# A fifth dB tile in the pool of the selective scan from the first image on, and one sz tile fewer in the stage that prepares the scan

## The chip, the cores and the metric

The kernel runs on one core of one Trainium2 chip. A run's time is the device time of one execution, in microseconds (us). Engines are named as in the profile: PE (TensorE, matmuls), DVE (VectorE), ACT (ScalarE), POOL (GpSimd) and SP (SyncE, which here only issues DMAs). "L534" is line 534 of the kernel.

## What is computed

Four images of 64x64 positions with 128 channels go through four layers: a state-space block (layer 0), a global attention (layer 1), a convolution block (layer 2) and a windowed attention with an MLP (layer 3). The change is in layer 0, whose core is a scan over the 4096 positions in four directions k, for 256 channels with 16 states each:

```
def step(h, t):
    x_t, d_t, B_t, C_t = t
    h = exp(d_t[..., None] * A) * h + (d_t * x_t)[..., None] * B_t[:, :, None, :]
    return (h, einsum('bkdn,bkn->bkd', h, C_t))
```

The names in the kernel are: dA for the exponential, du for d_t * x_t, dB for du times B, and hc for h times C.

## The kernel before, in words

**Two stages in one program.** `scan_inputs` (L307) works out, for one image, what the scan reads: a layer norm, a projection, a 3x3 convolution, the gate sz = silu(z), and for each direction delta, du and the rows B and C. All of it goes to scratch in DRAM. `selective_scan` (L487) reads that back and runs the scan of one image. `network` (L1751) calls `scan_inputs` for image 0, then the scan of image 0, and behind it in the text `scan_inputs` for images 1 to 3; then, for each later image, its scan and, in the text after it, the rest of the network (`rest`, L1721) for the image before. A scheduler fixes the order of each engine's queue when the program is built, by priorities and by an estimate of times: the scan's instructions have a lower priority (`SCAN_FIRST`, L1790) than the other stages, so that they fill what the others leave free. On the chip each queue runs strictly in that order.

**A unit of the scan.** For each of 4 directions, 8 chunks of 512 positions and 2 halves of the channels there are 4 groups of states (`j`, L523) and 2 tiles (`pp`, L531): 512 units for an image, 2048 in all. One unit is:

- one dB product on POOL (L534), 128x1024, from a du tile and the B rows, into a tile that `S.inputs.tile()` gives;
- two exponentials on ACT (L540), 128x512 each, into PSUM tiles dA, of which there are three;
- two scans on DVE (L542), 128x512 each, from dA and dB;
- the C product, either two 128x512 products on DVE (L547) or one 128x1024 product on POOL (L555);
- copies of the last state on ACT (L549, L551), and four of the matmuls on PE that sum over states (L588).

Which units have their C product on POOL is set by `ON_POOL` (L57): six of sixteen in image 0, seven of sixteen later. A product on POOL is put `BEHIND` = 2 units later in the text (L557), so its priority comes after the dB product two units on. The hc tile of a unit is free again when PE has read it.

**The tiles.** The class `Tiles` (L470) hands out tiles of [128, 2, 512] in turn from one pool, and, after `widen`, from a second pool too. hc has 6 tiles in image 0 and 10 later; dB has 4 in image 0 and 5 later. `widen` sets `turn` to -40 (L477), so that the first 40 tiles after it still come from the first pool alone. A dB product waits until the two scans that read the same tile before have ended.

```
    def widen(self, pool, extra):
        self.more, self.extra, self.turn = pool, extra, -40
...
                        dB = S.inputs.tile()
                        nc.gpsimd.tensor_mul(dB, dus[pp], mid(bt, 2))
```

**sz.** In `scan_inputs`, the pool `si_a` has two buffers for a tile unless a number is given. sz (L381) is written by two silu activations on ACT (L389) for each of the eight chunks of an image, and sent to DRAM by a DMA that ACT issues (L412).

Of the kernel before, what the change touches and what calls it, by code (L numbers as in the profile page):

```python
# [28 lines left out]
F32 = mybir.dt.float32  # L29
# [11 lines left out]
ND = DI // 128  # L41
FF = 4 * C
NF = FF // 128
LC = 512
# [242 lines left out]
def token_tiles(dram, c):  # L287

    return dram[span(c), :].rearrange("(t p) c -> p t c", p=128)
# [17 lines left out]
def scan_inputs(tc, K, A, D, img):  # L307
# [5 lines left out]
    with ExitStack() as ctx:  # L313
        pool = ctx.enter_context(tc.tile_pool(name="si_a", bufs=2))
# [49 lines left out]
        for c in range(NCH + 1):  # L364
            acts = []
            if c < NCH:
                xt = pool.tile([128, 4, 128], F32, name="x")
                nc.sync.dma_start(xt, token_tiles(A["x"][img], c))
                xnT = pool.tile([128, LC], F32, name="xnT")
                layernorm_T(tc, K, pool, psum, xt, ln_w, ln_b, xnT)  # L370
                band = pool.tile([128, ND, RC + 2, W], F32, name="band", bufs=3)
                bands[c] = band
                for d in range(ND):
                    ps = psum.tile([128, LC], F32, name="ps")
                    nc.tensor.matmul(ps, in_proj[:, d * 128 : (d + 1) * 128], xnT, start=True, stop=True)
                    rows = ps.rearrange("p (h w) -> p h w", w=W)
                    nc.scalar.copy(band[:, d, 1 : RC + 1, :], rows)
                    if c > 0:
                        nc.scalar.copy(bands[c - 1][:, d, RC + 1, :], rows[:, 0, :])
                        nc.scalar.copy(band[:, d, 0, :], bands[c - 1][:, d, RC, :])  # L380
                sz = pool.tile([128, ND, LC], F32, name="sz")  # L381
                for d in range(ND):
                    ps = psum.tile([128, LC], F32, name="ps")
                    mm = nc.tensor.matmul(
                        ps, in_proj[:, DI + d * 128 : DI + (d + 1) * 128], xnT, start=True, stop=True
                    )
                    if d == 0:
                        together.open(mm)
                    acts.append(lambda d=d, ps=ps, sz=sz: nc.scalar.activation(sz[:, d, :], ps, AF.Silu))  # L389
            if c > 0:  # L390

                b, src = c - 1, bands.pop(c - 1)
                top, bottom = (1 if b == 0 else 0), (RC + 1 if b == NCH - 1 else RC + 2)
                for d in range(ND):
                    ps = psum.tile([128, LC], F32, name="ps")
                    mm = conv3x3(
                        nc,
                        ps.rearrange("p (h w) -> p h w", w=W),
                        lambda t, d=d: diag[:, d, t, :],
                        src[:, d, top:bottom, :],  # L400
                        1 - top,
                        RC,
                        bottom - top,
                    )
                    acts.append(
                        lambda d=d, ps=ps, b=b: nc.scalar.activation(
                            xc[:, d, span(b)], ps, AF.Silu, bias=conv_b[:, d : d + 1]
                        )
                    )
            together.run(mm, acts)  # L410
            if c < NCH:
                nc.scalar.dma_start(D.sz[img][c], sz)  # L412
            if c > 0:
                nc.scalar.dma_start(D.xc[img][c - 1], xc[:, :, span(c - 1)])
                steps(0, c - 1)
# [24 lines left out]
def make_scan(ctx, tc, K, A):  # L440

    nc = tc.nc
    S = SimpleNamespace()
    big = ctx.enter_context(tc.tile_pool(name="ss_big", bufs=1))
    S.pool = ctx.enter_context(tc.tile_pool(name="ss", bufs=2))
    S.psum = ctx.enter_context(tc.tile_pool(name="ss_ps", bufs=1, space=PSUM))
    load = loader(tc, big, A, 0)
    S.A = load("A_log", [128, KD, NJS, NPR, 2])
    nc.scalar.activation(S.A, S.A, AF.Exp)
    nc.vector.tensor_scalar_mul(S.A, S.A, -1.0)  # L450
    ds4 = load("Ds", [128, ND, KD])
    total = big.tile([128, ND], F32, name="Dsum")
    nc.vector.tensor_reduce(total, ds4, AX.X, ALU.add)
    S.skip = big.tile([128, ND, 128], F32, name="skip_diag")
    for d in range(ND):
        nc.scalar.activation(S.skip[:, d, :], K.ident, AF.Copy, scale=total[:, d : d + 1])

    S.pick = big.tile([128, 32], F32, name="pick")
    nc.gpsimd.memset(S.pick, 1.0)
    for base, sign in ((0, 1), (3, -1)):  # L460
        nc.gpsimd.affine_select(
            S.pick, S.pick, [[-4 * sign, 32]], ALU.is_ge, 0.0, base=base, channel_multiplier=sign
        )
    S.unit = 0
    S.products = Tiles(S.pool, "hc", 6)
    S.inputs = Tiles(S.pool, "dB", 4)
    return S


# [1281 lines left out]
def network(tc, A, out):  # L1751
    nc = tc.nc
    with ExitStack() as ctx:
        nc.scalar.preload_act_table_set("natural_log_exp_and_others")
        K = make_consts(ctx, tc)
        dram = ctx.enter_context(tc.tile_pool(name="scratch", bufs=1, space=DRAM))

        def scratch(name, shape, kind=F32):
            return dram.tile(shape, kind, name=f"{name}_dram")

        D = SimpleNamespace()
        D.bias = scratch("bias", [len(BIAS_KINDS), 128, HEADS * 512])
        D.biasT = [[scratch(f"biasT{k}_{i}", [128, HEADS, LC]) for i in range(4)] for k in range(3)]
        D.T = scratch("T", [128, HEADS * (2 * KW - 1) + 1, W])
        D.conv_diag = scratch("conv_diag", [128, ND, 9, 128])
        D.w2_norms = scratch("w2_norms", [128, len(NORMS2), 4])
        D.w2_cv4, D.w2_bias = scratch("w2_cv4", [128, 128]), scratch("w2_bias", [3, 128], BF16)
        for name, shape in (("sz", [128, ND, LC]), ("xc", [128, ND, LC]), ("y", [128, ND, LC])):
            setattr(D, name, [[scratch(f"{name}{b}_{c}", shape) for c in range(NCH)] for b in range(B)])
        for name, shape in (("delta", [128, ND, LC]), ("du", [128, ND, LC]), ("bc", [NS, 2, LC])):  # L1770
            made = [
                [[scratch(f"{name}{b}_{k}_{c}", shape) for c in range(NCH)] for k in range(KD)] for b in range(B)
            ]
            setattr(D, name, made)
        D.y_first = [[[scratch(f"y_first{b}_{k}_{c}", [128, ND, LC]) for c in range(NCH)] for k in range(2)] for b in range(B)]
        D.y_cols = [scratch(f"y_cols{b}", [NCH, 128, NCH, ND, RC * RC]) for b in range(B)]
        for name in ("x4", "x5"):
            setattr(D, name, [scratch(f"{name}_{b}", [NT, C]) for b in range(B)])
        D.shift = [scratch(f"shift{b}", [NJ, 128]) for b in range(B)]

        with ExitStack() as scan_ctx:
            S = make_scan(scan_ctx, tc, K, A)
            make_conv_diagonals(tc, K, A, D.conv_diag)
            with priority(tc, K, SCAN_FIRST // 2):
                with tc.tile_pool(name="mk_w2", bufs=1, side="right") as pool:
                    make_layer2(tc, K, A, D, pool)
            scan_inputs(tc, K, A, D, 0)
            before = None
            for img in range(B):
                with priority(tc, K, SCAN_FIRST):  # L1790
                    selective_scan(tc, K, S, D, img)
                if img == 0:
                    make_bias(tc, K, A, D)
                    for later in range(1, B):
                        scan_inputs(tc, K, A, D, later)
                    more = scan_ctx.enter_context(tc.tile_pool(name="ss_more", bufs=1))
                    S.products.widen(more, 4)
                    S.inputs.widen(more, 1)
                else:
                    rest(tc, K, A, D, img - 1, before)  # L1800
                    before = img - 1, out[img - 1]
            rest(tc, K, A, D, B - 1, before, scan_ctx.close, out[B - 1])
        needed = ctx.enter_context(tc.tile_pool(name="needed", bufs=1)).tile([1, 1], mybir.dt.int32, name="needed")
        bound_exceeded(tc, K, needed)
        with tc.If(nc.values_load(needed) > 0):
            everything_again(tc, K, A, D, out)
# [80 lines left out]
```

## Time and profile before

| what | value |
|---|---|
| median of 3 runs | 8719.03 us (8716.36 to 8720.45) |
| the profiled execution's own time | 8713.75 us |
| its span, first to last instruction | 8712.4 us |
| POOL busy | 7119.3 us (82%) |
| DVE busy | 7095.9 us (81%) |
| PE busy | 6971.9 us (80%) |
| ACT busy | 5688.0 us (65%) |
| first dB product of image 0 starts | 102.4 us |
| last du product of `scan_inputs` starts | 2046.8 us |
| last scan of image 3 starts | 7620.1 us |
| dB products on POOL, L534 | 2048, 2367 ns each |
| C products on POOL, L555 | 864, 2367 ns each |
| du products on POOL, L358 | 128, 2614 ns each |

The span is 1.35 us less than the time of the same execution, and that time is 5.28 us below the median. A row of the profile's groups gives the line, the engine, the operation, what it writes and reads, the shapes and the count; then the busy time in us and the mean of one in ns; then the engine's idle time just before these instructions, and what ended most of it. The windows give, for stretches of the span, the busy time of each engine with its number of instructions, the granted clock of PE and the share and rate of the DMAs. After 7621 us the scan is over and POOL has nearly nothing to do; the rest of the network for image 3 takes what is left of the span.

### The profile page before, as it was taken

To read this page: it belongs to the slowest core of one execution; us is meant where nothing else is said; L and a number is where in the kernel's file an instruction comes from. 1 tells how busy PE (TensorE), PEld (TensorE's weight loads), DVE (VectorE), ACT (ScalarE), POOL (GpSimd) and SP (SyncE) were. 2 spreads that over 40 slices of the span, in tenths; PEclk is the share of its full clock that TensorE was granted. 3 is DMA by queue.
4 is the path that set the end of the run, shared out by engine and by line. 5 is a ranking of instruction groups with operands and counts; after the bars stand their busy time and mean duration, and the time that the engine had idled before them with its cause. 6 is when DMAs were issued, how large, how long until landed. Compare 5 with 4: busy or idle time off the path is not lost. (4 is left out here: it accounts for less than half of the span.)

```text
span 8712.4 us, 101929 instructions
## 1 busy us (share of the span) xinstructions
PE 6971.9 (80%) x30468; PEld 2615.3 (30%) x30468; DVE 7095.9 (81%) x8477; ACT 5688.0 (65%) x11652; POOL 7119.3 (82%) x3112
## 2 busy tenths in 40 slices
PE   6758587786788878777798877777899877888978
PEld 2223132222422222233322222234322223344333
DVE  4788787788899999998899999998899999913433
ACT  5657676675666676667766676667766766654366
POOL 6989999898899989998899989998899989900000
PEclk8868687787899988888899988888999988899989
DMA  5776667676555556565455566565455565520020
GB/s 181 254 261 236 244 235 257 227 261 220 172 176 167 170 190 206 190 223 186 162 180 169 171 197 201 192 225 176 164 172 168 180 204 196 191 73 5 0 84 11
DMA packets 859647, 1562.73 MB, mean 179 GB/s; under 512 B 224446, under 2 KB 342348, under 8 KB 856781
## 3 DMA queue, kind: packets, MB, share of 16 engines
q1 hardware_dynamic: 728781, 1379.94, 47.8%
q10 hardware_dynamic: 130304, 176.19, 5.7%
q8 instruction: 244, 4.00, 0.2%
q14 instruction: 318, 2.61, 0.1%
HBM read 1286.51 MB, written 281.92 MB: 180 GB/s over the span
## 5 line engine op out<-in xcount | busy, mean ns | idle before, releaser
L534 POOL TENSOR_TENSOR dB<-du,b_rows 128x1024 f32<-128x1024 f32 x2048 | 4797.9, 2367 | 374.9 <-DVE hc L542 95.0
L540 ACT ACTIVATE dA<-dt,w_A_log 128x512 f32<-128x512 f32 x4096 | 2778.3, 690 | 509.9 <-DVE hc L542 256.7
L542 DVE TENSOR_TENSOR_SCAN dA<-dA,state,dB 128x512 f32<-128x512 f32 x2072 | 2559.9, 1272 | 295.9 <-POOL dB L534 140.4
L555 POOL TENSOR_TENSOR hc<-hc,c_rows 128x1024 f32<-128x1024 f32 x864 | 2045.3, 2367 | 73.4 <-issue 22.2
L542 DVE TENSOR_TENSOR_SCAN hc<-dA,state,dB 128x512 f32<-128x512 f32 x1512 | 1871.9, 1267 | 281.8 <-ACT dA L540 123.5
L547 DVE TENSOR_TENSOR hc<-dA,c_rows 128x512 f32<-128x512 f32 x2368 | 1522.6, 675 | 31.8 <-PE py L588 13.9
L588 PE MATMUL py<-hc,pick 128*32 128x512 f32 x8192 | 1231.0, 675 | 261.5 <-POOL hc L555 235.4
L549 ACT COPY state<-dA 128x1 f32<-128x1 f32 x2072 | 318.6, 158 | 1170.8 <-DVE hc L547 1158.9
L878 PE MATMUL pa<-e,l_v 128*128 128x512 f32 x2048 | 1069.5, 654 | 16.6 <-ACT e L834 16.1
L830 PE MATMUL pair<-l_g,l_f 32*128 32x512 f32 x2048 | 533.3, 670 | 172.6 <-ACT e L834 130.6
L834 ACT ACTIVATE e<-pair 128x1024 f32<-128x1024 f32 (+1 forms) x448 | 508.5, 1135 | 234.4 <-PE pair L830 228.0
L1019 POOL MEMSET l_h<- 64x128 f32 x8 | 1.6, 196 | 707.9 <-DVE l_h L993 707.9
L878 PEld LDWEIGHTS pa<-e,l_v 128*128 128x128 f32 x2048 | 376.3, 200 | 673.9 <-issue 624.4
L588 PEld LDWEIGHTS py<-hc,pick 128*32 128x32 f32 x8192 | 212.1, 115 | 996.5 <-issue 467.5
L277 PE MATMUL ps<-band,w_conv_diag 128*128 128x504 f32 (+3 forms) x1152 | 501.9, 595 | 6.4 <-ACT delta L427 5.7
L1404 PE MATMUL pair<-table,ident 128*128 128x512 f32 x768 | 397.3, 641 | 91.7 <-ACT e L1414 63.3
L231 PE MATMUL ps<-ident,ln_xn 128*128 128x128 f32 x512 | 144.4, 375 | 327.6 <-ACT ln_xn L228 243.9
L542 DVE TENSOR_TENSOR_SCAN dA<-dA,dB 128x512 f32<-128x512 f32 x296 | 348.2, 1211 | 45.8 <-ACT dA L540 22.0
L358 POOL TENSOR_TENSOR du<-delta,xc 128x1024 f32<-128x1024 f32 x128 | 333.4, 2614 | 47.7 <-ACT delta L427 46.7
L1414 ACT ACTIVATE e<-pair 128x1024 f32<-128x1024 f32 (+1 forms) x224 | 254.3, 1135 | 95.8 <-PE pair L1408 95.5
L277 PEld LDWEIGHTS ps<-band,w_conv_diag 128*128 128x128 f32 x1152 | 221.1, 193 | 288.0 <-issue 261.1
L830 PEld LDWEIGHTS pair<-l_g,l_f 32*128 32x128 f32 x2048 | 140.0, 189 | 530.2 <-ACT e L834 258.9
(297 smaller groups left out, 8674.4 us busy)
## 6 DMA issues: line engine op xcount, KB each, us to landing
b_rows<-bc_dram SPq DMA_DIRECT2D x1024, 256.0 KB
c_rows<-bc_dram SPq DMA_DIRECT2D x1024, 256.0 KB
dt<-delta_dram SPq DMA_DIRECT2D x512, 512.0 KB
du<-du_dram SPq DMA_DIRECT2D x512, 512.0 KB
delta_dram<-delta ACTq DMA_DIRECT2D x128, 512.0 KB
du_dram<-du SPq DMA_DIRECT2D x128, 512.0 KB
table<-biasT_dram SPq DMA_DIRECT2D x72, 512.0 KB
y_first_dram<-y_sum ACTq DMA_DIRECT2D x128, 256.0 KB
```

Of the source, the lines that this page charges most:

```text
L277: mm = nc.tensor.matmul(out[:, r0 - row0 : r1 - row0, c0:c1], lhsT((dy + 1) * 3 + dx + 1), src[:, r0 + dy : r1 + dy, c0 + dx : c1 + dx], s ...
L358: nc.gpsimd.tensor_mul(du.rearrange("p d (a b) -> p d a b", b=H), deltas[b].rearrange("p d (a b) -> p d a b", b=H), tk,)
L534: nc.gpsimd.tensor_mul(dB, dus[pp], mid(bt, 2))
L540: nc.scalar.activation(dA, dts[pp][:, g, :], AF.Exp, scale=S.A[:, k, j, pr, g : g + 1])
L542: nc.vector.tensor_tensor_scan(hg[:, order], dA[:, order], dB[:, g, order], 0.0 if i == 0 else state[:, j, pr, g : g + 1], ALU.mult, ALU.add,)
L547: mm = nc.vector.tensor_mul(hc[:, g, :], dA, ct)
L555: made.append(nc.gpsimd.tensor_mul(hc, hc, mid(ct, 2)))
L588: mm = nc.tensor.matmul(py[0][32 * q : 32 * q + 32, :], S.pick, hcs[q // 2][:, q % 2, :], start=(k == 1 and j == 0), stop=(j == NJS - 1),)
L830: nc.tensor.matmul(ps[:, u, :], f[quad, t // 4, span(t % 4, 128)], g[quad, c, :], start=True, stop=True)
L834: made = nc.scalar.activation(e, ps, AF.Exp)
L878: nc.tensor.matmul(pa, v[:, 8 * q + t, :], es[q], start=(t == 0 and q == 0), stop=(t == 7 and q == 3),)
L1404: nc.tensor.matmul(ps[:, u, :], K.ident, t[:, u, :], start=True, stop=False)
```

## The change

The pool of the scan gets five dB tiles when it is made, before image 0. The second pool, which is opened after image 0, no longer holds a dB tile; it still holds the four extra hc tiles. In `scan_inputs` sz has one tile where it had two. A dB tile and an sz tile are of one size, 4 KB in each partition, so the room that the two stages take together stays what it was.

```diff
@@ scan_inputs
-                sz = pool.tile([128, ND, LC], F32, name="sz")
+                sz = pool.tile([128, ND, LC], F32, name="sz", bufs=1)
@@ make_scan
     S.products = Tiles(S.pool, "hc", 6)
-    S.inputs = Tiles(S.pool, "dB", 4)
+    S.inputs = Tiles(S.pool, "dB", 5)
@@ network
                     S.products.widen(more, 4)
-                    S.inputs.widen(more, 1)
```

## The prediction

> **What bounds the kernel now.** I read the page first: its busy digits, 40 slices of the span.
>
> ```profile
> DVE  4788787788899999998899999998899999913433
> POOL 6989999898899989998899989998899989900000
> ```
>
> POOL and DVE share the scan's load, and POOL is near full from the second slice until the scan ends. So I cut the span into the stages of the program, in the view of windows (length, then busy time of PE, weight loads, DVE, ACT and POOL with counts, PE's granted clock, DMA share and GB/s).
>
> ```profile
> 102.00:2050.00 1948.00, 1397.03 (x4439) 488.98 (x4437) 1529.00 (x1754) 1302.08 (x2924) 1819.10 (x778) 0.77 0.71 245
> 2050.00:2235.00 185.00, 130.56 (x541) 69.80 (x538) 167.66 (x226) 106.45 (x232) 148.80 (x64) 0.80 0.61 199
> 2235.00:4026.00 1791.00, 1480.78 (x6976) 534.53 (x6974) 1682.36 (x1954) 1203.72 (x2467) 1710.07 (x742) 0.89 0.57 187
> 7621.00:8713.00 1092.00, 931.73 (x4646) 426.16 (x4638) 363.58 (x575) 576.98 (x873) 1.49 (x5) 0.93 0.11 35
> ```
>
> From 102 to 2050 us the scan of image 0 runs beside the inputs of the later images. There POOL is busy 1819.10 of 1948 us (93%), DVE 1529.00 (78%): POOL is the bound, with 129 us idle. From 2050 to 2235 us the rest of image 0's scan runs alone, and DVE is the bound (167.66 of 185). The other images take about 1.8 ms each, POOL at 95%. The last 1092 us hold no scan. The images follow one another, so a microsecond saved in image 0's scan moves all behind it and the end.
>
> Next, the groups of those stages by line; first image 0 (102 to 2050 us), with four dB tiles:
>
> ```profile
> L534 POOL TENSOR_TENSOR dB<-du,b_rows 128x1024 f32<-128x1024 f32 x471 | 1102.0, 2358 | 112.1 <-PE ps L335 20.1 <-DVE hc L542 17.7 <-PE py L588 16.7
> L555 POOL TENSOR_TENSOR hc<-hc,c_rows 128x1024 f32<-128x1024 f32 x175 | 412.3, 2356 | 30.0 <-issue 9.3 <-PE ps L335 8.0 <-PE ps L347 7.5
> L542 DVE TENSOR_TENSOR_SCAN hc<-dA,state,dB 128x512 f32<-128x512 f32 x304 | 376.5, 1268 | 168.0 <-PE py L588 71.4 <-POOL dB L534 69.6 <-ACT dA L540 23.6
> ```
>
> then three stretches with five tiles: 2420 to 4006 us (image 1), 4006 to 5800 (image 2), 5800 to 7620 (image 3):
>
> ```profile
> L534 POOL TENSOR_TENSOR dB<-du,b_rows 128x1024 f32<-128x1024 f32 x461 | 1076.6, 2355 | 41.2 <-issue 13.7 <-DVE hc L542 12.6 <-DVE dA L542 4.3
> L534 POOL TENSOR_TENSOR dB<-du,b_rows 128x1024 f32<-128x1024 f32 x513 | 1202.9, 2373 | 75.4 <-DVE hc L542 25.0 <-issue 15.1 <-DVE dA L542 12.1
> L534 POOL TENSOR_TENSOR dB<-du,b_rows 128x1024 f32<-128x1024 f32 x512 | 1203.2, 2384 | 95.6 <-DVE hc L542 30.2 <-issue 19.9 <-DMA y_before<-xc_dram 7.2
> ```
>
> POOL's idle time stands mainly before dB products. What such a wait is, the timeline shows (start, duration, idle before it):
>
> ```profile
> 779.40 4.66 POOL L534 TENSOR_TENSOR dB<-du,b_rows 128x1024 f32<-128x1024 f32 x2
> ...
> 780.03 7.91 PE L277 MATMUL ps<-band,w_conv_diag 128*128 128x512 f32 x18
> ...
> 787.87 1.06 PE L588 MATMUL py<-hc,pick 128*32 128x512 f32 x6
> ...
> 788.95 2.46 DVE L542 TENSOR_TENSOR_SCAN hc<-dA,state,dB 128x512 f32<-128x512 f32 x2 [6.55 <-PE py L588]
> ...
> 791.55 2.38 POOL L534 TENSOR_TENSOR dB<-du,b_rows 128x1024 f32<-128x1024 f32 x1 [7.49 <-PE ps L335]
> ```
>
> The sums over hc (L588) stood behind 18 convolution matmuls in PE's queue; DVE waited 6.55 us for an hc tile; POOL, with all dB tiles full, started the next dB 0.14 us after the scans that began at 788.95 had ended (791.41). The releaser printed, a PE matmul, is not an input of L534: the wait is for the tile.
>
> **The change part by part.** It removes and adds no instruction; it moves waits.
>
> (1) Five dB tiles in image 0. While DVE stands still POOL can do one more dB, 2.36 us. The stall above is 7.49 us, so 2.36/7.49 = 31% of it goes. Over the stage: of the 112.1 us, 15.4 are the wait for the very first du load (the view of waits puts them to that DMA), which no tile shortens. That leaves 96.7 us before 470 products, 0.206 us each. With five tiles the rows give 41.2/461 = 0.089, 75.4/513 = 0.147 and 95.6/512 = 0.187. At these rates the stage would keep 42, 69 or 88 us, a gain of 55, 28 or 9 us. Bounds: at most 96.7; at least 0, since a dB done early only lets POOL come sooner to the next C product (L555), which waits for the same scan. I take the middle row, 28 us; 31% of 96.7, 30 us, agrees. Does it reach the end? A unit in this stage costs POOL 2.36 + 6/16 x 2.36 = 3.24 us, so 28 us are 8.6 units done before 2050 us; each would else cost DVE, the bound of the stretch after, two scans and 10/16 of two products, 2 x 1.27 + 1.25 x 0.675 = 3.38 us: 29 us. So it goes through at about one for one. DVE has 22% free in the stage to follow; late next is then PE's hold on hc tiles (71.4 us in the row above).
>
> (2) The first units of image 1. With `turn` at -40 they still have four tiles now; 2226 to 2420 us shows 21.8 us before 52 products. At 0.147 that would be 7.6, a gain of up to 14 us. But image 0's output starts in that stretch, and the bound there may be DVE; I count 0 and keep 14 for the range. The stretch 2050 to 2226 us has 28.7 us of such idle time, with DVE at 91%: 0.
>
> (3) One sz tile. The silu of a chunk now waits until the sz before has landed. In the timeline the closest pair is ACT's issue of L412 at 50.97 us and the next silu at 71.9, 20.6 us later; in the quiet stretch after 51 us its 128 packets have started by 54 us. Queued behind a late silu on ACT would be the silu of xc, on which the inputs hang, and the scan's exponentials. Cover of over 17 us: cost 0. In the stretch of heaviest DMA load (600 to 650 us, share 1.00) the next silu is over 24 us away; if one transfer outlived that, by some 10 us, ACT would stand for it once: 10 us at most.
>
> (4) Where dB tiles lie. Five in one pool, or four and one: the turn is the same, so 0 in images 1 to 3, as far as the order of the queues stays. That order is fixed anew for the whole program; no row prices it.
>
> A rule that speaks against more POOL work beside DVE: the dB rows have a mean of 2358 ns in image 0 and 2384 in image 3, at most 2474, and DVE's scan 1276 against 1271: neither stretches. The Trainium skill, "SBUF — State Buffer", section "Who interferes with whom", says that a DVE instruction with two SBUF inputs and a GpSimd instruction that reads SBUF block each other for a whole instruction. By it each dB moved beside such a DVE instruction would give back its gain, and the sum would be 0; L542 and L547 read dA from PSUM and one SBUF tile, which the rule exempts, and the rows agree.
>
> Sum of parts 1 to 4: -28 + 0 + 0 + 0 = -28 us. The profiled execution would go from 8713.75 to 8686; against the median, 5.28 us higher, 8719 - 28 = **8691 us** (-0.32%).
>
> **The rivals.** (A) Absorbed: POOL runs one dB ahead and waits at L555 instead, for the same scan. For it: of POOL's 22 operations in 16 units six are C products, and a queue in fixed order stops at the first. Against it: idle before L555 is no larger with five tiles (12.6 us in image 1, 30.0 in image 0). Gain 0 to 9: 8710 to 8719.
>
> (B) Slower: the extra dB stands ahead of a C product in POOL's order. The product is up to 2.36 us late, PE's sum with it, and with only six hc tiles in image 0 DVE waits longer. The place is in the waits of this stage:
>
> ```profile
> DVE hc L542 <- PE py L588: 85.4, 25, 9.1
> DVE hc L547 <- PE py L588: 13.4, 5, 3.3
> ```
>
> These 30 waits, each longer by 2.36 us, are 71 us; less 28, the kernel is 43 slower: 8762. It needs more than 12 of the 30 to lose at all, and 20 to be seen. Against it: a product comes due two units after its dB, and six hc tiles leave some three units of slack.
>
> (C) More: image 1's rate (55) and part 2 (14): -69, 8650.
>
> **How the numbers follow.** A measurement of this kernel tells 0.2%, 17 us, from no change. Forecast 0.45 (10 to 50 faster; nearly all over 17), C 0.05, A 0.25, B 0.25, which stands also for queues reordered to DVE's harm. Faster 0.50, same 0.25, slower 0.25. The forecast's own range is 8669 to 8702. The whole runs from just beyond C, 8645, to B with nearly all its waits, 8755.
>
> **What would show it.** Right: in 102 to 2050 us idle before L534 falls from 112 to about 84, more than 471 dB products start in it, and image 0's last scan ends near 2207 us, not 2235; images 1 to 3 keep 1.79, 1.785 and 1.81 ms. A: idle before L555 grows by what L534's loses. B: DVE's waits on L588 grow from 99 us. Part 3 is wrong if ACT idles before L389 on its DMA. The whole is wrong if images 1 to 3 change length, by reordered queues.

## The result, and the profile after

| | before | after |
|---|---|---|
| median of 4 runs each, us | 8719.74 | 8779.62 (8775.05 to 8783.06) |
| ratio, 95% interval | 1 | 1.0067 [1.0055, 1.0079] |
| span of the profiled execution, us | 8712.4 | 8773.0 |
| last scan of image 0 ends, us | 2235.4 | 2201.3 |
| last du product of `scan_inputs` ends, us | 2049.7 | 2155.2 |
| last scan of image 3 ends, us | 7621.4 | 7624.5 |

The kernel became 60 us slower; 28 us faster was forecast. The scan of image 0 did end about when the forecast said (2201 us; the forecast said about 2207). The kernel lost time elsewhere, in `scan_inputs`, whose end the prediction did not follow. The busy digits of the page after, for the lines shown of before:

```profile
DVE  4788788788899999998899999988899999713433
POOL 6999999999899999998799999998899999700000
```

They look much the same, and the last slice with work on POOL is the same one. The windows of after, cut where its stages end (columns as before):

```profile
102.00:2050.00 1948.00, 1390.47 (x4429) 482.90 (x4427) 1554.64 (x1780) 1290.64 (x2919) 1820.08 (x781) 0.76 0.71 241
2050.00:2156.00 106.00, 54.30 (x148) 13.43 (x148) 84.14 (x88) 58.32 (x121) 106.00 (x45) 0.60 0.77 263
```

POOL is busy 1820.08 us in the first stretch, as in before (1819.10): no idle time of POOL was won. Then follow 106 us in which POOL is busy without a break and the inputs of image 3 are still being made; in before they were done at 2050. The groups by line of after, 102 to 2050 us, beside the rows of before in the prediction, say what changed inside the same POOL time:

```profile
L534 POOL TENSOR_TENSOR dB<-du,b_rows 128x1024 f32<-128x1024 f32 x481 | 1127.6, 2368 | 136.9 <-DVE hc L542 66.2 <-issue 18.5 <-DMA du<-du_dram 15.7
L555 POOL TENSOR_TENSOR hc<-hc,c_rows 128x1024 f32<-128x1024 f32 x178 | 421.2, 2366 | 4.6 <-issue 2.4 <-DMA b_rows<-bc_dram 1.2 <-DVE hc L542 0.7
L358 POOL TENSOR_TENSOR du<-delta,xc 128x1024 f32<-128x1024 f32 x116 | 301.6, 2608 | 2.1 <-DMA du_dram<-du 1.7 <-ACT state L551 0.4
```

and the du products of before in the same stretch:

```profile
L358 POOL TENSOR_TENSOR du<-delta,xc 128x1024 f32<-128x1024 f32 x126 | 328.7, 2619 | 1.7 <-DMA du_dram<-du 0.9 <-ACT delta L427 0.7
```

The idle time before L534 and L555 together is 136.9 + 4.6 = 141.5 us; in before it was 112.1 + 30.0 = 142.1. It only moved from one line to the other. The scan got 10 dB and 3 C products more (481 for 471, 178 for 175), and `scan_inputs` got 10 du products fewer (116 for 126). The fifth tile did not fill idle time: it changed whose turn it is on a POOL that is full.

**Where POOL is full.** For each image `scan_inputs` ends with a phase that runs `steps(1, c)` for the eight chunks in column order (L416), 16 du products. POOL is the only engine that is busy nearly all the time there. Windows of the first two of these phases in before (373.0 to 509.3, 925.6 to 1065.4):

```profile
373.00:509.30 136.30, 70.46 (x212) 18.47 (x208) 97.49 (x99) 82.21 (x179) 135.35 (x57) 0.66 0.72 255
925.60:1065.40 139.80, 68.24 (x199) 16.45 (x197) 98.74 (x101) 78.32 (x173) 139.80 (x59) 0.56 0.68 242
```

and of the same phases in after:

```profile
362.10:531.30 169.20, 91.43 (x250) 21.59 (x246) 127.98 (x133) 96.38 (x215) 167.51 (x71) 0.57 0.69 241
958.70:1114.70 156.00, 71.86 (x223) 17.83 (x221) 118.22 (x121) 86.77 (x187) 156.00 (x66) 0.60 0.68 237
```

POOL's count rises from 57 to 71 and from 59 to 66, with 16 du products in each. The groups of the scan on POOL in the first phase, before (373 to 509 us, which leaves out the last 0.3 us and one dB product of the count above):

```profile
L534 POOL TENSOR_TENSOR dB<-du,b_rows 128x1024 f32<-128x1024 f32 x29 | 67.4, 2342 | 0.0
L555 POOL TENSOR_TENSOR hc<-hc,c_rows 128x1024 f32<-128x1024 f32 x11 | 25.8, 2344 | 0.0
```

and after (362 to 531 us, also one dB product short):

```profile
L534 POOL TENSOR_TENSOR dB<-du,b_rows 128x1024 f32<-128x1024 f32 x39 | 91.6, 2369 | 0.0
L555 POOL TENSOR_TENSOR hc<-hc,c_rows 128x1024 f32<-128x1024 f32 x15 | 35.5, 2368 | 0.0
```

From the first to the last du product of the four phases POOL runs 149 dB and 57 C products for 116 and 45. That is 45 products more, at 2.37 us 107 us; the four phases together take 658.0 us for 553.5, 104.5 more; and `scan_inputs` ends 105.5 us later. The three numbers agree: the stretches between the phases changed by -10.9, 11.1, 2.5 and -1.8 us, together 1 us.

**Why that is the kernel's time.** The timeline of SyncE shows what follows the last du. Before:

```profile
2049.68 0.33 SPq L362 DMA_DIRECT2D du_dram<-du  x1
2050.06 0.42 SPq L196 DMA_DIRECT2D w_onorm_w<-in_L_conv_onorm_w  x1
```

and after:

```profile
2153.39 2.21 SPq L362 DMA_DIRECT2D du_dram<-du  x2
2155.65 0.42 SPq L196 DMA_DIRECT2D w_onorm_w<-in_L_conv_onorm_w  x1
```

The next instruction loads a weight of `scan_output`: the rest of the network for image 0 begins the moment `scan_inputs` ends, and not when the scan of image 0 ends. Its work starts there too. The prediction read the stretch behind 2050 us as the scan alone; the groups of before from 2050 to 2226 us, with the scan of image 0 still running, hold this row of `scan_output`:

```profile
L651 PE MATMUL ps<-y,center 128*128 128x512 f32 x32 | 17.4, 689 | 11.2 <-DVE center L634 11.2
```

And the rest stages follow one another directly: in before the last store of image 2's stage is issued at 7657.34 us and the first load of image 3's at 7659.76. Windows between the starts of the four rest stages (a start is the stage's first instruction in any queue, a wait counted), before:

```profile
2050.00:3857.00 1807.00, 1488.38 (x6992) 542.51 (x6988) 1700.55 (x1960) 1199.08 (x2455) 1720.77 (x746) 0.88 0.57 187
3857.00:5780.00 1923.00, 1575.29 (x7294) 570.26 (x7290) 1785.49 (x2091) 1305.02 (x2688) 1817.10 (x788) 0.89 0.57 187
5780.00:7657.00 1877.00, 1562.53 (x7190) 577.54 (x7190) 1707.12 (x2013) 1267.21 (x2597) 1727.37 (x749) 0.89 0.55 180
```

and after:

```profile
2156.00:3949.00 1793.00, 1473.89 (x6980) 533.13 (x6980) 1683.16 (x1938) 1188.43 (x2438) 1709.89 (x742) 0.88 0.56 186
3949.00:5863.00 1914.00, 1559.14 (x7242) 569.29 (x7242) 1760.13 (x2070) 1296.17 (x2662) 1796.86 (x779) 0.89 0.57 185
5863.00:7717.00 1854.00, 1528.28 (x7094) 562.60 (x7094) 1635.73 (x1943) 1232.94 (x2527) 1648.28 (x715) 0.90 0.54 175
```

So the sum of the chain is, in us: 2050 + 1807 + 1923 + 1877 + 1056 = 8713 before, and 2156 + 1793 + 1914 + 1854 + 1056 = 8773 after. 106 us are lost at the start of the chain and 46 given back along it. A likely reason for the 46, which no run tests, is that the scan is 34 units further on when the chain starts (505 dB products have started for 471), so that less of DVE's time in the chain goes to the scan: DVE's busy time in the three rows sums to 5193 us before and 5079 after. In before the last scan ends 36 us before the chain reaches the last image, in after 92 us.

### The profile page after: what moved, and what is told of

Read it like the earlier page. It is cut to its first block, busy times and chain, and to the rows that moved or that the text cites. A ratio compares the mean times of both kernels' runs of the same rounds, so it can differ in the third digit from the quotient of the medians.

```text
span 8773.0 us, 101931 instructions
## 1 busy us (share of the span) xinstructions
PE 6956.3 (79%) x30468; PEld 2598.0 (30%) x30468; DVE 7092.7 (81%) x8477; ACT 5681.5 (65%) x11652; POOL 7117.5 (81%) x3112
## 5 line engine op out<-in xcount | busy, mean ns | idle before, releaser
L534 POOL TENSOR_TENSOR dB<-du,b_rows 128x1024 f32<-128x1024 f32 x2048 | 4818.7, 2391 | 402.1 <-DVE hc L542 164.2
L555 POOL TENSOR_TENSOR hc<-hc,c_rows 128x1024 f32<-128x1024 f32 x864 | 2065.3, 2390 | 47.8 <-ACT state L551 11.7
L547 DVE TENSOR_TENSOR hc<-dA,c_rows 128x512 f32<-128x512 f32 x2368 | 1523.8, 676 | 58.6 <-PE py L588 24.1
L588 PE MATMUL py<-hc,pick 128*32 128x512 f32 x8192 | 1226.3, 676 | 239.6 <-POOL hc L555 211.8
L277 PE MATMUL ps<-band,w_conv_diag 128*128 128x504 f32 (+3 forms) x1152 | 500.2, 593 | 3.9 <-ACT delta L427 3.1
L588 PEld LDWEIGHTS py<-hc,pick 128*32 128x32 f32 x8192 | 210.7, 115 | 985.5 <-issue 478.9
L542 DVE TENSOR_TENSOR_SCAN hc<-dA,dB 128x512 f32<-128x512 f32 x216 | 254.8, 1207 | 60.4 <-PE py L588 29.9
```

Of the source, the lines that this page charges most:

```text
L277: mm = nc.tensor.matmul(out[:, r0 - row0 : r1 - row0, c0:c1], lhsT((dy + 1) * 3 + dx + 1), src[:, r0 + dy : r1 + dy, c0 + dx : c1 + dx], s ...
L542: nc.vector.tensor_tensor_scan(hg[:, order], dA[:, order], dB[:, g, order], 0.0 if i == 0 else state[:, j, pr, g : g + 1], ALU.mult, ALU.add,)
L547: mm = nc.vector.tensor_mul(hc[:, g, :], dA, ct)
L555: made.append(nc.gpsimd.tensor_mul(hc, hc, mid(ct, 2)))
L588: mm = nc.tensor.matmul(py[0][32 * q : 32 * q + 32, :], S.pick, hcs[q // 2][:, q % 2, :], start=(k == 1 and j == 0), stop=(j == NJS - 1),)
```

## The experiments

**The theories.** *Queue theory*: the fifth tile puts more scan work ahead of du products in POOL's fixed order, `scan_inputs` ends later, and the chain of rest stages carries this to the end. Rivals: *sz theory* (one sz tile stalls ACT); *hc theory* (rival B of the prediction: DVE's waits for hc tiles; in 102 to 2050 us they did grow, from 85.4 + 13.4 to 141.9 + 22.4 us); *scan theory* (POOL's scan sets the end, and the rest stages only fill gaps).

All runs, profiled executions in us; the "phases" are the four column-order phases, "chain" is the start of image 3's rest stage. A ratio is to runs of before on the same chip; before itself took 8713 to 8724 us on the chips used.

| kernel | phases | `scan_inputs` ends | scan of image 0 ends | scan of image 3 ends | chain | median | ratio to before, 95% interval |
|---|---|---|---|---|---|---|---|
| before | 553.5 | 2049.7 | 2235.4 | 7621.4 | 7656.6 | 8719.74 | |
| after | 658.0 | 2155.2 | 2201.3 | 7624.5 | 7716.9 | 8779.62 | 1.0067 [1.0055, 1.0079] |
| e1_sz1 | 552.6 | 2049.7 | 2234.6 | 7622.5 | 7657.9 | 8715.67 | 0.9999 [0.9990, 1.0009] |
| e3_dB3 | 481.0 | 1962.4 | 2271.5 | 7674.1 | 7623.4 | 8704.79 | 0.9985 [0.9975, 0.9994] |
| e4_after_du_dve | 544.6 | 2038.8 | 2278.2 | 7675.9 | 7608.9 | 8718.39 | 1.0001 [0.9991, 1.0010] |
| e6_before_du_dve | 528.1 | 2022.9 | 2246.9 | 7652.9 | 7620.2 | 8689.82 | 0.9969 [0.9958, 0.9981] |
| cut_before | 553.9 | 2052.3 | 2237.4 | 7627.1 | 7639.4 | 8696.98 | 0.9967 [0.9954, 0.9979] |
| cut_after | 658.3 | 2158.2 | 2204.1 | 7624.2 | 7686.8 | 8745.39 | 1.0024 [1.0014, 1.0034] |
| g2_gate4 | 563.7 | 2039.0 | 2233.1 | 7614.0 | 7558.1 | 8658.82 | 0.9925 [0.9908, 0.9941] |
| h3b_gate3 | 479.5 | 1983.8 | 2263.9 | 7685.5 | 7593.5 | 8711.92 | 0.9985 [0.9976, 0.9995] |
| g5_inverse | 629.3 | 2130.6 | 2201.5 | 7643.1 | 7718.4 | 8788.30 | 1.0082 [1.0065, 1.0099] |
| g3_wide | 566.1 | 2070.5 | 2199.7 | 7610.3 | 7684.1 | 8743.43 | 1.0035 [1.0021, 1.0049] |
| p_before | 500.2 | 2004.3 | 2148.2 | 7557.6 | 7575.1 | 8638.43 | 0.9912 [0.9895, 0.9928] |
| p_after | 532.3 | 2056.8 | 2177.6 | 7601.3 | 7654.8 | 8702.52 | 0.9980 [0.9971, 0.9990] |

Take for each kernel the later of the two times "scan of image 3 ends" and "chain": what comes after it is nearly constant. In the nine kernels where the chain is later, the span ends 1055.5 to 1069.2 us after it; in the five where the scan of image 3 is later (e3, e4, e6, g2, h3b), 1029.3 to 1041.9 us after that. So whichever of the two is later sets the end. And in twelve of the fourteen kernels the first load of the rest stage of image 0 is issued 0.4 us after the last du product has ended (4 us in p_before, 12 us in p_after).

**e1: one sz tile alone** (before, with the first edit only).

```diff
-                sz = pool.tile([128, ND, LC], F32, name="sz")
+                sz = pool.tile([128, ND, LC], F32, name="sz", bufs=1)
```

> Only the second half of the change: one sz tile, and dB tiles as before (4, then 5 from image 1). Queue theory (the fifth dB tile lets POOL's fixed order put more scan work ahead of the du products, scan_inputs ends later, and the chain of the rest stages behind it sets the end): POOL's order stays that of before, scan_inputs ends near 2050 us, the kernel takes 8720 +- 10 us. sz theory (the silu waits for the sz transfer, which delays scan_inputs): scan_inputs ends near 2155 us and the kernel takes about 8780 us.

`scan_inputs` ends at 2049.7 us and the kernel is level with before. The sz theory falls: one sz tile alone costs nothing that can be told (the interval of the ratio allows 9 us), and the loss came with the fifth dB tile. Five dB tiles beside two sz tiles were not run.

**e3: three dB tiles in image 0** (before, changed).

```diff
-    S.inputs = Tiles(S.pool, "dB", 4)
+    S.inputs = Tiles(S.pool, "dB", 3)
-                    S.inputs.widen(more, 1)
+                    S.inputs.widen(more, 2)
```

> The other direction: 3 dB tiles in image 0 (5 from image 1 on, as before), two sz tiles. Queue theory: among the du products of the four column-order phases there are 93 dB and 35 C products in POOL's queue, where before had 116 and 45; 33 x 2.36 = 78 us less, so scan_inputs ends near 1972 us, and the rest stages of image 0 start as much earlier. Image 0's scan ends later than 2235 us, by 20 to 50 us, and the scan of image 3 too; then the scan and no more the rest chain sets the end: 8700 to 8740 us. Tile theory (a dB tile more saves POOL idle time and one less costs it, and the slowdown has another cause): scan_inputs ends no earlier than 2050 us, and the kernel is slower by 40 us or more.

With three, four and five tiles `scan_inputs` ends at 1962, 2050 and 2155 us. The kernel with fewer tiles is a little faster, although the scan of image 0 ends 36 us later. Now the scan of image 3 ends last (7674 us, the chain 7623). The tile theory falls.

**e4, e6: the column-order du products on DVE**, in after and in before.

```diff
-                nc.gpsimd.tensor_mul(
+                (nc.vector if o == 1 else nc.gpsimd).tensor_mul(
```

> After, with the du products of the column-order steps (64 of 128) on DVE instead of POOL. Queue theory: these du products no longer stand behind dB and C products, scan_inputs ends at 2050 us or earlier, and the kernel takes 8720 us or less (POOL is also rid of 64 x 2.63 = 168 us). If the slowdown came from one sz tile, or from DVE's waits for hc tiles (99 us before, 174 us after), scan_inputs ends near 2155 us again, or the kernel stays over 8760 us, the more so as DVE gets 64 products more.

> Before, with the same 64 du products on DVE. Queue theory: POOL's 116 dB and 45 C products no longer delay du; scan_inputs ends some 50 to 100 us before 2050 us, the rest chain moves up as much, and the kernel takes 8640 to 8700 us, bound by whichever of the chain and the scan of image 3 ends last. If DVE is the tighter engine, its 64 products of 1.4 us or more (90 us) come back in the scan: 8720 us or more.

In e4 `scan_inputs` ends at 2039 us, 116 earlier than in after, and the kernel is level with before, though the fifth tile is there and DVE has more to do. Two things limit this. DVE's waits on L588 in 102 to 2050 us fell as well, to 100.4 us (164.3 in after, 98.8 in before), so e4 alone does not part the queue theory from the hc theory. And its fair partner with four tiles is e6, which is 29 us faster: with du on DVE the fifth tile still costs, there by the scan of image 3, which ends last in both (7675.9 and 7652.9 us). Against the hc theory stands the first stage of after itself: with the waits 65.5 us longer, the scan of image 0 ended 34 us earlier, and it is POOL's products that fill the phases. In e6 the kernel's time falls in the stated range, but `scan_inputs` ends only 27 us earlier, where 50 to 100 were expected: a du product costs DVE far more than the 1.4 us assumed (last section), and now DVE is the engine that is nearly full in the phases (512.3 of 528.1 us).

**cut: work left out of the rest stage of image 0.** In its windowed attention half of the keys of four chunks are not looked at.

```diff
             for i, group in enumerate(key_groups(c)):
+                if img == 0 and c < 4:
+                    group = group[: (len(group) + 1) // 2]
```

> Before, with work left out of the rest stages of image 0: in its windowed attention half of the keys of four of the eight chunks are not looked at (scores, exponentials and sums over them fall away). That shortens a stage in the shadow of image 1's scan by some 100 to 150 us. Chain theory: in before the chain of rest stages ends (7657 us) only 23 us behind the last scan plus its sums (7634), so the kernel gains little over that, 20 to 60 us: 8660 to 8700 us. Scan theory (POOL's scan sets the end, the rest stages only fill gaps): under 20 us, unless the scan itself gets faster by the missing contention.

> After, with the same keys left out. Chain theory: in after the chain ends at 7717 us, 88 us behind the last scan and its sums (7629), so the cut is worth 80 to 120 us: 8660 to 8700 us, within 20 us of the same cut of before, and nearly all of the 60 us between after and before is gone. Scan theory: the difference of 60 us between after and before stays.

What was left out was worth less than estimated: that attention takes 580.9 us for 619.7 in after, 609.2 for 624.5 in before. cut_before lies just inside its range (8697 us). cut_after does not: of the gap of 60 us to the same kernel with four tiles 48 stay, where under 20 were expected, so as a measure of the gap this pair misses. What it shows is the chain: in cut_after the scan of image 3 ends as in after (7624.2 and 7624.5), the chain reaches the last image 30 us earlier, and the span is 25 us shorter (8748.1 for 8773.0). Of the 39 us taken out of the attention 25 reach the end, with the scan's end unmoved. The scan theory, by which the rest stages only fill gaps, falls.

**g2 and g5: the fifth tile outside the phases only, and inside them only** (both after, changed). Units of image 0 are counted by `S.unit`; the fifth tile is a pool of its own and is taken every fifth unit.

```diff
-    S.inputs = Tiles(S.pool, "dB", 5)
+    S.inputs = Tiles(S.pool, "dB", 4)
+    S.fifth = ctx.enter_context(tc.tile_pool(name="ss_fifth", bufs=1))
+    S.four = ((56, 103), (195, 242), (315, 362), (435, 482))
-                        dB = S.inputs.tile()
+                        four = S.unit % 5 or any(a <= S.unit < b for a, b in S.four)
+                        dB = S.inputs.tile() if four else S.fifth.tile([128, 2, LC], F32, name="dB")
```

In g5 the condition is `S.unit % 5 or (S.unit < 512 and not any(...))`.

> After, with the fifth dB tile in use only outside the four column-order phases: inside them (units 56-102, 195-241, 315-361, 435-481 of image 0) four tiles are taken in turn. One sz tile, five dB tiles as in after elsewhere. Among the du products of these phases POOL's queue now has 120 dB and 46 C products (before 116 and 45, after 149 and 57). Queue theory: scan_inputs ends at 2050 to 2075 us and the kernel takes 8705 to 8735 us, with image 0's scan ending at 2235 us or earlier. If the fifth tile hurts wherever it is (hc tiles, DVE), it stays over 8750 us.

> The opposite of g2_gate4: in image 0 the fifth dB tile is in use only inside the four column-order phases (units 56-102, 195-241, 315-361, 435-481) and four tiles elsewhere; five from image 1 on. POOL's queue has 139 dB and 57 C products among the du products of these phases (before 116 and 45). Queue theory: 35 x 2.36 = 83 us more, scan_inputs ends near 2130 us, and the kernel takes 8740 to 8785 us, nearly all of the loss of after. If the loss comes from the fifth tile elsewhere, or from the kernel's order of queues as a whole, it takes under 8735 us or over 8800.

`scan_inputs` ends at 2039 us with the tile outside the phases, and at 2131 us, as worked out, with the tile inside them. g5 is as slow as after, a little more than expected. So the lateness of `scan_inputs` comes from those 188 units. But g2 is 46 us faster than the range given: its chain is shorter behind `scan_inputs` too (image 0's rest stage takes 1744 us for 1807), and that part is not explained.

**g3: the same with wider stretches of four tiles**, (56, 110), (190, 250), (310, 370), (430, 490).

> As g2_gate4, with wider stretches of four tiles (units 56-109, 190-249, 310-369, 430-489). 120 dB and 46 C products among the du products, so scan_inputs ends at 2045 to 2080 us. If the time of g2_gate4 (8659) comes from keeping the column-order phases short and the tile elsewhere, it is 8640 to 8690 us again; if the quick rest stage of image 0 there (1744 us for 1807 in before) was an accident of the queues' order, it is 8695 to 8745 us.

The phases are as short as in g2 (566.1 and 563.7 us), yet the kernel is 85 us slower than g2 (96 by the ratios, each to its own chip): `scan_inputs` ends 31 us later, and image 0's rest stage takes 1791 us. The quick rest stage of g2 is not a property of the phases; by the expectation on record it was an accident of the queues' order. What in that order made it quick is open.

**h3b: three tiles inside, five outside** (stretches (56, 99), (190, 235), (305, 350), (420, 465); the other two tiles in a pool of their own).

> Five dB tiles outside the four column-order phases and three inside (units 56-98, 190-234, 305-349, 420-464), one sz tile. POOL's queue has 93 dB and 36 C products among the du products of these phases. Queue theory: scan_inputs ends at 1960 to 1985 us as with three tiles throughout, image 0's scan earlier than the 2271.5 us that it had there; the end is then set by the scan of image 3: 8675 to 8705 us, the fastest so far or level with the 8705 of three tiles throughout.

`scan_inputs` ends where it should (1984 us), the scan of image 3 ends last (7685 us), and the kernel is 7 us over the range. The phases cannot be pressed further with profit: the scan then sets the end.

**p: no C product on POOL in the phases**, in before and in after; the units of the phases use L547 on DVE.

```diff
-                        on_pool = S.unit % 16 in ON_POOL[img > 0]
+                        on_pool = S.unit % 16 in ON_POOL[img > 0] and not any(
+                            a <= S.unit < b for a, b in ((56, 103), (195, 242), (315, 362), (435, 482)))
```

> Before, with no C product on POOL in the four column-order phases of image 0 (units 56-102, 195-241, 315-361, 435-481): these C products go to DVE, which is 70% busy there. POOL's queue has 119 dB and no C products among the du products of these phases (before 116 and 45): 42 x 2.36 = 99 us less, so scan_inputs ends near 1955 us (1940 to 1975), while the scan has started 478 units by then (before 470). Queue theory: the rest chain moves up by some 90 us and the scan of image 0 ends earlier too, so the kernel takes 8600 to 8670 us, less than before and after. If DVE is the tighter engine there, the scan takes it back: 8700 us or more.

> After (five dB tiles, one sz tile), with the same C products on DVE. 128 dB and no C products among the du products (after 149 and 57, before 116 and 45): 33 x 2.36 = 78 us less than before, scan_inputs ends near 1972 us (1955 to 1995), and the kernel takes 8610 to 8690 us: about 100 us less than after, and the fifth tile is then worth within 30 us of four. If the fifth tile hurts in another way than by POOL's queue, it is slower than the same with four tiles by 40 us or more.

p_before is, level with g2, the fastest kernel of the study, 0.9912 of before: `scan_inputs` ends 45 us earlier (99 were expected; POOL is no longer full in the phases, 457.5 of 500.0 us) and the scan of image 0 ends 87 us earlier, so both candidates for the end moved. p_after is 77 us faster than after, but 64 us slower than p_before, and its `scan_inputs` ends 85 us later than worked out from POOL's counts. By the expectation on record a cost of 40 us or more means that the fifth tile hurts in another way too. Of the 52 us by which `scan_inputs` ends later in p_after than in p_before, 32 lie in the phases: 21 are POOL's busy time (478.4 us for 457.5, 128 dB products for 119), and 11 are POOL's idle time, nearly all before du products (33.3 us for 21.6; in the first phase 19.2 us are put down to the store of an earlier du). So POOL's count explains 21 of the 52 us; the other part, and how 52 us become 64 at the end, are not explained.

## Why the prediction was wrong, point by point

- **What bounds the kernel.** The step that failed is the sentence "The images follow one another, so a microsecond saved in image 0's scan moves all behind it and the end". The scan of image 0 ended 34 us earlier and the kernel 60 us later. Two chains run side by side: the scans, and `scan_inputs` with the rest stages. In before the second ends last, by 36 us, so the end went with `scan_inputs`, which ended 105.5 us later. Two readings of the windows went with it. From 2050 to 2235 us the scan of image 0 does not run "alone": the rest stage of image 0 starts there. And the row from 7621 us on was taken as the work behind the scan; 36 us of it were the end of image 2's rest stage.
- **The scan's own chain.** There too the saved time did not reach the end. The scans of images 1 to 3 took 1797.0, 1804.8 and 1821.4 us, for 1790.8, 1784.4 and 1810.8 in before; so the scan of image 3 ended 3 us later, not 34 earlier. The prediction had asked for equal lengths there as a sign that it was right. Why they grew is open.
- **Part 1, the fifth tile.** The gain in image 0 was put at 28 us and measured 34, but not by the way given, so that the two are close is luck. POOL's idle time stayed (142.1 and 141.5 us), moving from L555 to L534 where the prediction had it shrink before L534 from 112 to about 84; it grew to 136.9. The 10 dB products more were paid for by 10 du products. The bound "at least 0" held for the scan of image 0 and not for the kernel, since the prediction counted what the scan wins on POOL and not what loses its turn: 45 products of 2.37 us among the du products, 107 us.
- **Part 2 and part 3.** Part 2, the first units of image 1, was left at 0 and is not told apart in any run. Part 3, one sz tile, cost 0 as said (e1).
- **Part 4, the order of the queues.** It was named as not priced, and in the range only as a share of B. Kernels with phases of nearly one length (g2, g3) lie 85 us apart, so the range was too narrow for a kernel whose queues are ordered anew. (Within it "10 to 50 faster" and "8669 to 8702", which is 17 to 50 faster, do not agree; nothing turns on it.)
- **Rival A** had POOL's idle time right in sum, which stays, and wrong in direction: it expected the idle time to go from L534 to L555; L534's grew by 24.8 us and L555's fell by 25.4. For the kernel it forecast a gain of 0 to 9 us.
- **Rival B** gave the right sign. Its waits grew by 65.5 us in 102 to 2050 us, but image 0's scan ended earlier all the same. The operation whose lateness counted was not the C product but du.
- **Still open.** Shown are the count of POOL's products in the phases, the end of `scan_inputs`, and that the later of the two chains sets the end. Not shown is what the chain takes behind `scan_inputs`: from its end to the start of image 3's rest stage the kernels without left-out work take 5519 (g2) to 5661 us (e3), and the rest stage of image 0 alone 1744 to 1846. So the 105 us at the end of `scan_inputs` are explained, and that 60 of them are left at the end is measured, not derived. Open is also what the fifth tile costs in p_after and e4 beyond POOL's count.

## What to carry to other kernels

Where a background stage shares a full engine with the work in front, a buffer more for the background was here a larger share of that engine, not a better use of it: count the other stage's instructions in the same stretch before and after. Before a gain in one stage is carried to the end, look at what the first instruction of the next stage waits for; here one line of SyncE's timeline showed that the rest of the network starts with the end of `scan_inputs` and not of the scan. When two chains end within 36 us of each other in 8.7 ms, a gain in the one that ends last is worth about 36 us at most by itself, and a gain in the other nothing.

## What the runs showed of the hardware

A du product of 128x1024 with both inputs in SBUF took DVE 1.89 to 1.93 us in e6 where POOL did nothing beside it, and 3.08 in the mean. The instructions on the tile delta on DVE, in e6 (least, median and largest ns):

```profile
L358 DVE TENSOR_TENSOR du<-delta,xc x64: 1861/2755/10702, 372.4 to 2020.8; 128x1024 f32<-128x1024 f32 x64
```

The mean is more than the 2856 ns that POOL took for a du product in the first column-order phase of before. The timeline of e6 shows how the two meet: once with DVE's product first, once with POOL's dB first, and once with POOL's products back to back.

```profile
996.99 1.86 DVE L358 TENSOR_TENSOR du<-delta,xc 128x1024 f32<-128x1024 f32 x1
997.20 3.87 POOL L534 TENSOR_TENSOR dB<-du,b_rows 128x1024 f32<-128x1024 f32 x1 [3.11 <-issue]
...
464.88 2.34 POOL L534 TENSOR_TENSOR dB<-du,b_rows 128x1024 f32<-128x1024 f32 x1
465.00 3.99 DVE L358 TENSOR_TENSOR du<-delta,xc 128x1024 f32<-128x1024 f32 x1
...
911.47 6.96 POOL L534 TENSOR_TENSOR dB<-du,b_rows 128x1024 f32<-128x1024 f32 x3
911.79 10.70 DVE L358 TENSOR_TENSOR du<-delta,xc 128x1024 f32<-128x1024 f32 x1 [2.91 <-DMA du_dram<-du]
918.40 2.33 POOL L555 TENSOR_TENSOR hc<-hc,c_rows 128x1024 f32<-128x1024 f32 x1
```

The one that starts first takes its own time, and the other ends about its own time after it: POOL's product took 3.87 us for the usual 2.36, DVE's 3.99 for 1.9. In the third case DVE's product ended 1.76 us after the last of four POOL products in a row. L547 on DVE, with one input in PSUM, stays at 677 ns for half the size, with the same POOL work beside it. The Trainium skill, "SBUF — State Buffer", section "Who interferes with whom", says that a DVE instruction with two SBUF inputs contends with a GpSimd instruction that reads SBUF, and that one with at most one SBUF input, outside the 2-port modes, does not; this run agrees. So moving work from a full POOL to DVE cost time on both when its inputs lay in SBUF, though e6 as a whole was faster than before (0.9969). The C products of p_before, whose input dA lies in PSUM, moved without that price (677 ns on DVE, dB on POOL 2360).
